# Weights in larger pieces and a re-planned start in a four-layer graph network kernel

## The chip, the cores and the metric

The kernel runs on one core of a Trainium2 chip. The metric is the device time of one execution in microseconds (us). The time before is the median of three runs; the profile is of one further execution. The engines are TensorE (PE; PEld is its loading of the stationary operand), VectorE (DVE), ScalarE (ACT), GpSimd (POOL) and SyncE (SP), which here only issues transfers (SPq).

## The reference

128 graphs of 128 nodes with 512 features pass four layers in float32. Each layer is `x = layernorm(x + f(x))`; the adjacency `adj` is the same in all four.

```python
# layer 0: Ah = adj + I, d = rowsum(Ah)**-0.5
f = relu((d * Ah * d) @ x @ W0 + b0)
# layer 1
q, k = split(x @ Wqk.T);  v = x @ Wv.T
w = softmax_over_nodes(sum((q @ k.T / 8) * adj, -1))
f = w * v
# layer 2
f = relu(concat([x, (adj @ x) / rowsum(adj)]) @ W2.T)
# layer 3: the d * Ah * d of layer 0
f = (d * Ah * d) @ (x @ W3 + b3)
```

## The kernel before

The graphs are worked on in 32 groups `t` of four. A group's x stays in one on-chip tile, `x_t`, through all four layers. Groups overlap: while group `t` is in layers 0 and 1, group `t - 1` is in layers 2 and 3.

Every product of 512 x 512 weights is done by `project` in a scheme with seven half-size products in place of eight (Strassen in Winograd's form). The weights' two row halves `h` and two column halves `j` give B11 (h=0, j=0), T1 (first loaded with the block h=0, j=1), B21 (h=1, j=0) and B22 (h=1, j=1); `weight_sums` makes T1, T2, T3 and T4 out of them in place, four subtractions for each weight, on VectorE for Wv and on GpSimd for the others. `left_sums` makes the matching sums of the left operand (`agg0s`, `xT1s`, `agg2s`, `xT2s`, `agg3s`). `project` emits the products in the order B11, B21, T1, T2, B22, T3 (layer 1 has B21 after T1), and T4 in a function `tail` that is kept in the list `tails` and runs within a later product. Three PSUM regions are used: B11 and B21 add up in the first, T1 and B22 in the second, T2, T3 and T4 in the third. ACT copies the first region (`s_o`, `s_v`) between B11 and B21, and VectorE reads the second and third (`u_o`, `u_v`) before the next product adds to them. `hooks` put other work behind a named product.

`w[:, k, c]` is the weight block of product `k` and row chunk `c`, 256 contiguous columns; each matrix is loaded in four blocks, for Wv and the x half of W2 (`turned`) each in four transfers of 32 partitions.

A matrix product needs its left operand transposed. `aggregate` gets that for free (x is the stationary operand, the transposed adjacency the moving one), and ACT copies the result from PSUM. Where x itself is wanted transposed, there are two ways: `turn_x` writes x to DRAM and reads it back in pieces (`xT1s`, `xT1y`), of which VectorE transposes blocks of 32 x 32; `turn_on_tensor` copies x on ACT, transposes it on TensorE by the identity, and ACT copies the result from PSUM. `begin` uses the second for group 0, `prep_transpose` for the adjacencies of groups 0 and 1; later adjacencies go through DRAM as well (`sa`, `ya`).

The order of work is set at build time. `Plan` records every operation; TensorE's order is that of the program text. `schedule` then lists the others one by one: for each engine, the ready operation with the earliest due time, by estimated durations. Its estimate for transfers is a latency LAND and one shared bus of BUS elements of 4 bytes per ns. At run time each engine takes its instructions strictly in the listed order and waits on semaphores. All transfers are issued on SyncE's one queue. All recorded operations carry line 266 in the profile.

Of the kernel before, what the change touches and what calls it, by code (L numbers as in the profile page):

```python
# [10 lines left out]
FP = mybir.dt.float32  # L11
AF = mybir.ActivationFunctionType
ALU = mybir.AluOpType
AX = mybir.AxisListType

P = 128
K = 32
Q = P // K
# [3 lines left out]
H = F // 2  # L22
# [103 lines left out]
class Plan:  # L126
# [4 lines left out]

    ENGINES = ("tensor", "vector", "scalar", "gpsimd", "sync")
    HOP = 200
    LAND, BUS = 1600, 95

    def __init__(self, nc, est):
        self.nc, self.est, self.ops, self.tags, self.group, self.dram = nc, est, [], {}, None, None
# [57 lines left out]
    def schedule(self):  # L195
        number = {op: i for i, op in enumerate(self.ops)}
        for (_, tag, bufs), tiles in self.tags.items():
            used = []
            for t in sorted((t for t in tiles if t.ops), key=lambda t: number[t.ops[0]]):
                if len(used) == bufs:  # L200
                    old = used.pop(min(range(bufs), key=lambda i: number[used[i].ops[-1]]))
                    assert number[old.ops[-1]] < number[t.ops[0]], (tag, bufs)
                    for op in t.ops:
                        if op.preds.isdisjoint(t.ops):
                            op.preds.update(old.ops)
                used.append(t)
        now = 0
        for op in self.ops:
            assert all(number[p] < number[op] for p in op.preds)
            for p in op.preds:  # L210
                p.succs.append(op)
            if op.engine == "tensor":
                op.last = now
                now += op.dur
        for op in reversed(self.ops):
            due = min([s.last - self.hop(op, s) for s in op.succs], default=now)
            op.last = min(op.last, due - op.dur)
        queue = {e: [] for e in self.ENGINES}
        waiting = {op: len(op.preds) for op in self.ops}
        free, bus, port = dict.fromkeys(self.ENGINES, 0), 0, 0  # L220
        pe = [op for op in self.ops if op.engine == "tensor"]
        for op in self.ops:
            if not op.preds:
                queue[op.engine].append((0, number[op], op))
        done = []
        while len(done) < len(self.ops):
            best = None
            for e in self.ENGINES:
                q = queue[e]
                if e == "tensor":  # L230
                    q = [c for c in q if c[2] is pe[0]]
                if not q:
                    continue
                q = [(max(c[0], port if c[2].port else 0),) + c[1:] for c in q]
                at = max(free[e], min(c[0] for c in q))
                pick = min((c for c in q if c[0] <= at), key=lambda c: (c[2].last, c[1]))
                for c in q:
                    if at < c[0] < at + pick[2].dur and c[2].last < at + pick[2].dur and c[2].last < pick[2].last:
                        pick, at = c, c[0]
                if best is None or at < best[0]:  # L240
                    best = at, e, pick[2]
            at, e, op = best
            queue[e] = [c for c in queue[e] if c[2] is not op]
            op.start, op.end = at, at + op.dur
            free[e] = op.end
            if op.port:
                port = op.end
            if e == "sync":
                bus = max(bus, op.end + self.LAND) + op.size / self.BUS
                op.lat = max(op.lat, bus - op.end)  # L250
            if e == "tensor":
                pe.pop(0)
            done.append(op)
            for s in op.succs:
                waiting[s] -= 1
                if not waiting[s]:
                    queue[s.engine].append((max(p.end + self.hop(p, s) for p in s.preds), number[s], s))
        return done
# [48 lines left out]
def kernel(  # L307
# [16 lines left out]
    last = NT - 1  # L324
# [31 lines left out]
    def weight(src, name, queue, turned=False):  # L356


        w = const.tile([P, 7, 2, H], FP, tag=name, name=name)
        for h in range(2):  # L360
            for j in range(2):
                s = src[:, j * H:(j + 1) * H]
                if turned:
                    s = s.rearrange("(b h c k) m -> h b k c m", b=Q, h=2, c=2)[h]
                    for b in range(Q):
                        queue.dma_start(w[b * K:(b + 1) * K, 2 * h + j], s[b])
                else:
                    queue.dma_start(w[:, 2 * h + j], s.rearrange("(h c p) m -> h p c m", h=2, c=2)[h])
        return w

    def weight_sums(w, eng):
        eng.tensor_tensor(w[:, T3], w[:, B22], w[:, T1], ALU.subtract)
        eng.tensor_tensor(w[:, T1], w[:, T1], w[:, B11], ALU.subtract)
        eng.tensor_tensor(w[:, T2], w[:, B22], w[:, T1], ALU.subtract)
        eng.tensor_tensor(w[:, T4], w[:, B21], w[:, T2], ALU.subtract)

    def broadcast_row(src, name, queue):
        r = const.tile([P, F], FP, tag=name, name=name)
# [136 lines left out]
    def project(name, t, parts, first, c11, fin, hooks=None, after=lambda: None, early=True,  # L515
                when=lambda f: f(), pairs=(0, 1)):

        hooks = hooks or {}  # L520
        qs = slice(pairs[0], pairs[-1] + 1)

        def region():
            return ps_b.tile([P, 2, H], FP, tag="pb", name=f"p_{name}_{t}")[:, qs]

        def operand(left_, k):
            s = st[left_, t]
            if isinstance(s, Ref):
                return s.rearrange("p (q r) (h c) n -> p q r h c n", r=2, h=2)[:, :, 0, (B11, B21).index(k)]
            return s[k]  # L530

        def product(p, k, fresh):
            with nc.unit():
                for q in pairs:
                    for i, (left_, w) in enumerate(parts):
                        for c in range(2):
                            nc.tensor.matmul(p[:, q - pairs[0], :], operand(left_, k)[:, q, c, :], w[:, k, c, :],
                                             start=(fresh and q == pairs[0] and i == 0 and c == 0),
                                             stop=(i == len(parts) - 1 and c == 1), skip_group_check=True)
            for f in hooks.get(k, ()):  # L540
                f()

        def block(tag):
            return tp.tile([P, 2, H], FP, tag=tag, name=f"{tag}_{name}_{t}", bufs=1 if tag in ("u5", "sb") else 2)[:, qs]

        g, q, v = region(), None, None
        product(g, B11, True)
        sa, sb = first(g, block)
        finish_tails()
        if early:  # L550
            product(g, B21, False)
            when(lambda: c11(g, block))
        q = region()
        product(q, T1, True)
        u5 = block("u5")
        nc.vector.tensor_tensor(u5, q, sb, ALU.add)
        if not early:
            product(g, B21, False)
            when(lambda: c11(g, block))
        v = region()  # L560
        product(v, T2, True)
        u2 = block("u2")
        nc.vector.tensor_tensor(u2, v, sb, ALU.add)
        product(q, B22, False)
        nc.vector.tensor_tensor(u2, q, u2, ALU.add)
        when(lambda: (fin(0, 1, u2), norm_stats(name, t, 0, pairs)))
        product(v, T3, False)
        nc.vector.tensor_tensor(u5, v, u5, ALU.add)
        fin(1, 1, u5)

        def tail():
            product(v, T4, False)
            nc.vector.tensor_tensor(sa, v, sa, ALU.add)
            fin(1, 0, sa)
            norm_stats(name, t, 1, pairs)
            after()

        tails.append(tail)
# [56 lines left out]
    def l0_agg(t, eng=nc.gpsimd, pairs=(slice(0, 2),)):  # L635
        left("agg0", t)
        for g in range(G):
            aggregate("agg0", t, g, st["anT", t])
        left_sums("agg0", t, eng, pairs)
# [189 lines left out]
    def begin():  # L829
# [3 lines left out]
        weight_sums(w0_sb, nc.gpsimd)  # L833
        l0_agg(0, nc.vector, ONE_BY_ONE)
        prep_rows(1)
        l0_out(0, {B11: [lambda: prep_transpose(1)], B22: [lambda: l0_agg(1)]})
        weight_sums(wv_sb, nc.vector)
        l0_out(1)
        l1_turn(0, turn_on_tensor, (0,))
# [3 lines left out]
        l1_qk(0, 1)  # L843
        for w in (w2x_sb, w2a_sb, w3_sb):
            weight_sums(w, nc.gpsimd)
        l1_turn(1)
        l1_out(0, {B11: [lambda: l1_scores(0)], B21: [lambda: l1_softmax(0)], T3: []})
        finish_tails()
        for r in range(2):
            l1_qk(1, r)  # L850
        l2_both(0, 0)

    def prep(t):
# [23 lines left out]
            l2_agg(t, 0)  # L877

    l2_both(last, 0)
    for q in range(2):  # L880
        l2_out(last, {B21: [lambda: l2_both(last, 1)]} if q == 0 else {}, (q,))
    for q in range(2):
        l3_agg_pair(last, q, nc.gpsimd)
        l3_bias(last, (2 * q, 2 * q + 1))
# [34 lines left out]
```

## Time and profile before

| | before |
|---|---|
| time, median of 3 runs | 2489.22 us (2488.04 to 2489.28) |
| span of the profiled execution | 2486.8 us |
| TensorE busy | 2457.3 us, 99% |
| VectorE, ScalarE, GpSimd busy | 73%, 39%, 54% |
| TensorE's share of the chain that ended last | 97% |
| moved by DMA | 243.34 MB, mean 98 GB/s |

In a row of a timeline the first number is the start in us from the start of the span, the second the length of the row (which may hold several instructions, xN); then the engine, the line, the operation, what it writes and reads, and, in brackets, the idle time of that engine before the row and what released it. A float32 matmul of the text counts as two in a row: the four of one product appear as x8.

The loads of the start stand in this order on the queue: adjacency 0, x of group 0, adjacency 1, W0, b0, x of group 1, Wqk, Wv, W2, then adjacency and x of group 2, W3, b3.

### The profile page before, as it was taken

What the parts mean: (1) busy time and instruction counts of PE and PEld (TensorE: products, weight loads), DVE (VectorE), ACT (ScalarE), POOL (GpSimd) and SP (SyncE); (2) the same over time, 40 slices, a digit from 0 to 9 for tenths busy, and PEclk for the clock granted to TensorE, in tenths of its full rate; (3) what the DMA queues carried; (4) which work ended last, traced back from release to release, by engine and by line L of the source; (5) the groups of instructions that cost most, each with busy time, mean ns of one, the idle gap of its engine ahead of it and who ended that gap; (6) DMA issues with size and microseconds to landing.
All of it is one profiled execution on the core that took longest, in us unless ns stands there. A gap on an engine that the chain in (4) does not pass through costs nothing.

```text
span 2486.8 us, 37083 instructions
## 1 busy us (share of the span) xinstructions
PE 2457.3 (99%) x13470; PEld 2206.9 (89%) x13470; DVE 1810.0 (73%) x3169; ACT 973.2 (39%) x1981; POOL 1334.0 (54%) x1522
## 2 busy tenths in 40 slices
PE   8899999999999999999999999999999999999998
PEld 7789988989999899899899998998898999989987
DVE  6677777777777777777777777777777777777665
ACT  2334434343344343343433443433434434443335
POOL 5446555555556464555555564645555555645443
PEclk9999999999999999999999999999999999999999
DMA  5333434333344324343243443343442434423220
GB/s 178 69 93 81 108 88 123 111 78 101 98 106 123 94 77 109 91 124 110 72 107 93 112 123 88 79 111 93 123 110 68 112 90 115 118 81 86 77 60 34
DMA packets 398805, 243.34 MB, mean 98 GB/s; under 512 B 140832, under 2 KB 365600, under 8 KB 398624
## 3 DMA queue, kind: packets, MB, share of 16 engines
q1 hardware_dynamic: 398624, 240.98, 36.2%
q8 instruction: 107, 1.75, 0.3%
q14 instruction: 74, 0.61, 0.1%
HBM read 127.66 MB, written 113.25 MB: 97 GB/s over the span
## 4 chain that ended last, share of the span: by engine, by line
PE 97%; SPq 1%; DVE 1%; DMA 1%; ACT 0%; issue 0%; POOL 0%; ACTq 0%; POOLq 0%; DVEq 0%
PE p_o L266 61%; PE p_v L266 16%; PE p_agg L266 14%; PE p_qk L266 5%; PE p_sc L266 1%; SPq L266 1%; DMA x<-in_x_dram 0%; DVE x L266 0%; PE p_ws L266 0%; ACT xT L266 0%; PE p_w L266 0%; DMA adj<-in_adj_dram 0%; PE p_xT L266 0%; ACT agg L266 0%; DVE wv_sb L266 0%
## 5 line engine op out<-in xcount | busy, mean ns | idle before, releaser
L266 ACT COPY agg<-p_agg 128x512 f32<-128x512 f32 x384 | 221.3, 584 | 573.1 <-PE p_agg L266 573.1
L266 PE MATMUL p_o<-w_sb,agg 128*128 128x256 f32 x1536 | 353.4, 379 | 0.5 <-DVE u_o L266 0.5
L266 PEld LDWEIGHTS p_o<-w_sb,agg 128*128 128x128 f32 x1536 | 286.7, 190 | 37.3 <-DVE u_o L266 0.9
L266 PE MATMUL p_o<-w2x_sb,xT2s 128*128 128x256 f32 x1024 | 263.0, 379 | 3.1 <-DVE xT2s L266 3.1
L266 PE MATMUL p_o<-w2a_sb,agg2s 128*128 128x256 f32 x1024 | 262.8, 379 | 0.0
L266 POOL TENSOR_TENSOR xT1s<-xT 128x512 f32<-128x512 f32 x64 | 94.1, 1471 | 290.2 <-DVE xT L266 220.1
L266 PE MATMUL p_agg<-anT,x 128*128 128x128 f32 x2048 | 243.9, 277 | 0.3 <-DVE anT L266 0.3
L266 PE MATMUL p_o<-w_sb,agg0s 128*128 128x256 f32 x1024 | 230.0, 383 | 7.0 <-DVE u_o L266 5.9
L266 PEld LDWEIGHTS p_agg<-anT,x 128*128 128x128 f32 x2048 | 235.4, 192 | 1.3 <-DVE anT L266 0.6
L266 PE MATMUL p_v<-wv_sb,xT1s 128*128 128x256 f32 x1024 | 233.3, 381 | 0.0
L266 POOL TENSOR_TENSOR agg3s<-agg 128x512 f32<-128x512 f32 x62 | 84.1, 1357 | 272.3 <-ACT agg L266 272.3
L266 PEld LDWEIGHTS p_o<-w_sb,agg0s 128*128 128x128 f32 x1024 | 193.5, 192 | 34.2 <-POOL mro L266 4.9
L266 PEld LDWEIGHTS p_o<-w2x_sb,xT2s 128*128 128x128 f32 x1024 | 194.4, 190 | 29.9 <-DVE xT2s L266 3.6
L266 PE MATMUL p_o<-w_sb,agg3s 128*128 128x256 f32 x992 | 219.2, 379 | 0.0
L266 PEld LDWEIGHTS p_o<-w2a_sb,agg2s 128*128 128x128 f32 x1024 | 194.6, 190 | 26.5
L266 PEld LDWEIGHTS p_v<-wv_sb,xT1s 128*128 128x128 f32 x1024 | 189.6, 190 | 27.3
L266 PEld LDWEIGHTS p_o<-w_sb,agg3s 128*128 128x128 f32 x992 | 188.5, 190 | 25.6
L266 ACT ACTIVATE x<-x,nmro,rstdo 128x512 f32<-128x512 f32 x257 | 198.7, 809 | 4.8 <-ACT nmro L266 0.3
L266 PE MATMUL p_o<-w2x_sb,xT 128*128 128x256 f32 x768 | 197.5, 380 | 1.2 <-ACT s_o L266 0.7
L266 PE MATMUL p_o<-w2a_sb,agg 128*128 128x256 f32 x768 | 197.1, 379 | 0.0
L266 DVE TENSOR_TENSOR u_o<-p_o,s_o 128x512 f32<-128x512 f32 (+1 forms) x132 | 89.2, 675 | 145.3 <-PE p_o L266 145.3
L266 PE MATMUL p_v<-wv_sb,xT 128*128 128x256 f32 x768 | 181.6, 379 | 0.9 <-DVE u_v L266 0.9
(141 smaller groups left out, 4662.1 us busy)
## 6 DMA issues: line engine op xcount, KB each, us to landing
x<-in_x_dram SPq DMA_DIRECT2D x31, 1024.0 KB, 5.1
xT1s<-x SPq DMA_DIRECT2D x124, 256.0 KB, 2.5
xT1y<-xT1s SPq DMA_DIRECT2D x248, 128.0 KB, 3.3
out_dram<-x SPq DMA_DIRECT2D x31, 1024.0 KB, 5.4
xT2s<-x SPq DMA_DIRECT2D x120, 256.0 KB, 2.6
xT2y<-xT2s SPq DMA_DIRECT2D x240, 128.0 KB, 2.8
sa<-ana SPq DMA_DIRECT2D x120, 128.0 KB, 3.3
ya<-sa SPq DMA_DIRECT2D x120, 128.0 KB, 3.2
```

What stands on the lines that cost most here:

```text
L266: getattr(getattr(self.nc, op.engine), method)(*[v.real() if isinstance(v, Ref) else v for v in args], **{k: v.real() if isinstance(v, Ref ...
```

## The change

The weights are laid by row chunk first (`w[:, c, k]`), so that the two column halves of a row lie side by side, and each transfer takes whole rows: half as many transfers, of twice the size, with runs of 2 KB in place of 1 KB. The planner's figures for transfers are changed (LAND 1800, BUS 62 elements or 248 bytes per ns, and at most FLIGHT 9 transfers in flight), which moves the order of operations on VectorE, ACT, GpSimd and SyncE. Group 1's x for layer 1 is transposed on TensorE, as group 0's is, and its place is behind T3 of layer 1 of group 0. The preparation of group 1's adjacency moves from behind B11 to behind B21. At the end, T4 of layer 3 of the last group but one is held back until the second half of the last group's layer 2 operands has been prepared.

```diff
-    LAND, BUS = 1600, 95
+    LAND, BUS, FLIGHT = 1800, 62, 9
...
+            if e == "sync" and len(landed) >= self.FLIGHT:
+                at = max(at, landed[-self.FLIGHT])
...
             if e == "sync":
                 bus = max(bus, op.end + self.LAND) + op.size / self.BUS
                 op.lat = max(op.lat, bus - op.end)
+                landed.append(op.end + op.lat)
...
-        w = const.tile([P, 7, 2, H], FP, tag=name, name=name)
+        w = const.tile([P, 2, 7, H], FP, tag=name, name=name)
         for h in range(2):
-            for j in range(2):
-                s = src[:, j * H:(j + 1) * H]
-                if turned:
-                    s = s.rearrange("(b h c k) m -> h b k c m", b=Q, h=2, c=2)[h]
-                    for b in range(Q):
-                        queue.dma_start(w[b * K:(b + 1) * K, 2 * h + j], s[b])
-                else:
-                    queue.dma_start(w[:, 2 * h + j], s.rearrange("(h c p) m -> h p c m", h=2, c=2)[h])
+            to = w[:, :, 2 * h:2 * h + 2].rearrange("p c j m -> p c (j m)")
+            if turned:
+                for b in range(Q):
+                    queue.dma_start(to[b * K:(b + 1) * K], src.rearrange("(b h c k) m -> h b k c m", b=Q, h=2, c=2)[h][b])
+            else:
+                queue.dma_start(to, src.rearrange("(h c p) m -> h p c m", h=2, c=2)[h])
...
-        l0_out(0, {B11: [lambda: prep_transpose(1)], B22: [lambda: l0_agg(1)]})
+        l0_out(0, {B21: [lambda: prep_transpose(1)], B22: [lambda: l0_agg(1)]})
...
-        l1_turn(1)
-        l1_out(0, {B11: [lambda: l1_scores(0)], B21: [lambda: l1_softmax(0)], T3: []})
+        l1_out(0, {B11: [lambda: l1_scores(0)], B21: [lambda: l1_softmax(0)],
+                   T3: [lambda: l1_turn(1, turn_on_tensor), lambda: l1_qk(1, 0)]})
         finish_tails()
-        for r in range(2):
-            l1_qk(1, r)
+        l1_qk(1, 1)
         l2_both(0, 0)
...
     l2_both(last, 0)
+    held = tails.pop()
     for q in range(2):
-        l2_out(last, {B21: [lambda: l2_both(last, 1)]} if q == 0 else {}, (q,))
+        l2_out(last, {B21: [lambda: l2_both(last, 1), held]} if q == 0 else {}, (q,))
```

The indices in `weight_sums` and in `project` follow the new layout.

## The prediction before the run

> **What bounds the kernel now.** I read the page first, then TensorE's own timeline, then all engines around its waits. The page gives the bound:
>
> ```profile
> PE 2457.3 (99%) x13470; PEld 2206.9 (89%) x13470; DVE 1810.0 (73%) x3169; ACT 973.2 (39%) x1981; POOL 1334.0 (54%) x1522
> ...
> PE 97%; SPq 1%; DVE 1%; DMA 1%; ACT 0%; issue 0%; POOL 0%; ACTq 0%; POOLq 0%; DVEq 0%
> ```
>
> TensorE is busy 2457.3 of 2486.8 us and is 97% of the chain that ended last. The order of its instructions is written out by hand, so the change can gain only where TensorE stands idle or runs slowly. Its timeline over the first 110 us has these waits (the bracket is the idle time before the row):
>
> ```profile
> 23.60 1.99 PE L266 MATMUL p_o<-w_sb,agg0s 128*128 128x256 f32 x8 [1.34 <-DVE u_o L266]
> ...
> 37.09 3.74 PE L266 MATMUL p_o<-w_sb,agg0s 128*128 128x256 f32 x16 [1.01 <-POOL agg0s L266]
> 45.37 6.32 PE L266 MATMUL p_o<-w_sb,agg0s 128*128 128x256 f32 x16 [4.53 <-DVE u_o L266]
> ...
> 77.66 5.44 PE L266 MATMUL p_qk<-wqk_sb,xT 128*128 128x128 f32 x32 [3.88 <-DVE xT L266]
> ...
> 90.44 1.13 PE L266 MATMUL p_o<-w2x_sb,xT 128*128 128x256 f32 x4 [0.68 <-ACT s_o L266]
> ...
> 98.33 1.13 PE L266 MATMUL p_o<-w2x_sb,xT2s 128*128 128x256 f32 x4 [1.51 <-DVE xT2s L266]
> ...
> 2439.57 1.13 PE L266 MATMUL p_o<-w2x_sb,xT2s 128*128 128x256 f32 x4 [1.58 <-DVE xT2s L266]
> ```
>
> With 1.56 at 15.59, 0.85 at 71.78 and smaller ones (0.35, 0.16, 0.24, 0.29) that is 16.4 us of idle TensorE between 1.34 and 98.33 us, then none until 2429. Two rows are also slow: 16 matmuls take 6.32 us at 45.37 where the same form takes 3.74 at 37.09, and 32 of 128 columns take 5.44 where 32 of p_agg take 3.73. The second half of each gap shows as a lower clock in the table of stretches: 0.83 for 40 to 60, against 1.00 in 20 to 40. Together 2.6 + 1.7 = 4.3 us. So some 21 us can be won at the start, and a few at the end; 2330 us between are matmuls without a gap.
>
> What makes the 4.53 us wait stands in the timeline of all engines:
>
> ```profile
> 30.93 0.69 DVE L266 TENSOR_TENSOR u_o<-p_o,u_o 128x512 f32<-128x512 f32 x1 [1.87 <-PE p_o L266]
> ...
> 35.92 0.69 DVE L266 TENSOR_REDUCE deg<-adj 128x4 f32<-128x512 f32 x1 [4.29 <-DMA adj<-in_adj_dram]
> ...
> 37.58 3.43 DVE L266 TENSOR_TENSOR wv_sb<-wv_sb 128x512 f32<-128x512 f32 x2
> ...
> 44.55 0.68 DVE L266 TENSOR_TENSOR u_o<-p_o,sb_o 128x512 f32<-128x512 f32 x1
> ```
>
> VectorE works in order. It stood 4.29 us at the row sums of group 2's adjacency, whose load sat behind 36 weight transfers on the one queue, and the read of p_o that frees TensorE came last. In the same way the 3.88 us wait ends with four VectorE block transposes of group 1's x, which come after the normalization of group 0.
>
> [...] its half-clock stretches last 6.83 and 3.41 us, and follow the gaps of 4.53 and 3.88, none of 1.6 or less. [...] wv_sb at 37.58 takes 1.7 us each beside GpSimd sums, x<-u_o 0.68 alone. [...] the first loads here land in the order of issue.
>
> **The change, part by part.** I compared the order of each engine's instructions before and after, and walked through the start with durations of the trace; times below are TensorE's, before and then after.
>
> *Weights in larger pieces.* The 36 wv and w2 transfers before adj become 18 with twice the bytes. Before, issues were 0.47 us apart (wv from 16.5 to 22.5). Eighteen take about 8.5 us from 16.5, so adj is issued near 25, not 33.0, and lands (2.9) near 28. TensorE's and GpSimd's operands are the same 256 contiguous columns. The first w0 half now goes ahead of group 1's adjacency: 0.26 MB lands per 0.7 us (9.8, 10.5 for the w0 pieces), so adj lands at 10.4, not 9.05. The prep of group 1 is therefore hooked after B21. No gain: B21 now waits for the copy of B11 (0.7), and the sums agg0s still finish at 21.1, because each VectorE sum alternates with a GpSimd weight sum (1.45 us a pair) until then.
>
> *First B22 product (23.60).* VectorE's order puts a pair of sums (0.75) and an addition to x (0.65) before the read that frees the region: 23.54 + 1.4 + 0.1, so 25.2. A loss of 1.6. T1 of group 1 follows after the same work (12.5 us, and no 1.01 wait as only one weight sum stands before agg0s): 37.09 to 37.7.
>
> *Second B22 (45.37).* adj no longer blocks and one wv sum instead of two stands in the way. VectorE: T3 read from 32.5; x 34.9; wv 36.3; deg 37.0; s_o 37.7; small ones 38.2; x beside GpSimd 39.9; statistics 40.6; read 41.2. TensorE arrives at 37.7 + 3.45 = 41.2. The 4.53 wait and its slow clock go: 51.52 becomes 44.65 and, the same work following, p_ws (70.71) becomes 63.85.
>
> *Group 1's x on TensorE.* Adds 16 transposes: 8 take 1.04 us alone, 0.95 in a row, so 1.9 us. It takes away four block transposes (2.49) and twelve transfers. But T4 of layer 1 needs VectorE's last read of v, which now stands after group 0's additions and statistics: ws 64.3, two from p_v 65.4, two from u_v beside GpSimd 68.4 (2.96 before), statistics 69.9, read 70.6. TensorE would be there at 68.0. So T4 70.6 against 71.78, and layer 2's first aggregation 74.1 against 82.94. After that three waits grow, since their causes moved less than TensorE: ACT's copies of xT (0.29 to about 0.9; 86.05 to 77.8), s_o, now queued behind a normalization and two copies (0.68 to 1.2; 90.44 to 82.7), and xT2s. For the last, VectorE now has group 2's block transposes of ya ahead of agg2s. In before, ana was done at 87.6 and ya issued until 93.8, landing 3.2 later: 9.4 us. Ana is done at 78.6 now, ya lands near 88.0, and six instructions of 0.7 follow: 92.2 for 98.33, with a gap of 3.1 where 1.51 was. **Gain at the start 6.1 us.**
>
> *New figures for the planner.* They change the order on VectorE, GpSimd, ACT and the queue in every one of the some 29 steady periods of 76.1 us. I set the new places against what TensorE waits for at 1200 to 1276: the second half of xT for layer 1 is transposed at about 1254 instead of 1250.1, used at 1259.4; its sum s1 is ready at 1256.4, used at 1263.7; xT2s s1 moves from 1228.2 to 1228.6, used at 1236.7; a store of 1 MB (5.4) now goes ahead of xT1y, still in time. The least slack is some 2.5 us. Nothing.
>
> *The held tail.* T4 of group 30's layer 3 (1.73 us) moves into the 1.58 us gap before 2439.57. But it had hidden ACT's copy s_o, which B21 now waits for (0.6 to 0.7, like 90.44). Net **0.9 us**.
>
> Sum 7.0 us: 2489.2 - 7.0 = **2482.2**.
>
> **The rivals.** *Within 0.2%:* the new waits (3.1 before B22, 2.6 at T4, 3.1 at xT2s) [...] one of them a little longer costs its excess and about 2 us at half clock. Or ya lands 2 us later. Gain 2 to 5: about 2485.5. For it: two of three such gaps did this before. [...] 25%. *More:* ya lands early enough that xT2s waits 1.5 as before (1.6 more), the additions in front of T4 run without GpSimd (1.5), s_o fits at the end (0.6): 2478.5. For it: VectorE's order beside GpSimd decides. Against: all three at once. 7%. *Slower:* one new wait in each steady period, such as xT1y behind the store. At 0.5 us more than its slack in 29 periods it is 14.5 - 7.0: 2497. For it, the one queue is shared and VectorE blocks in order; against, slack of 2.5 us or more at each use. 6%.
>
> **How the numbers follow.** Forecast 62%, within 25%, more 7%, slower 6%. "Faster by over 0.2%" is below 2484.2: 62 + 7, 69%. The range takes in the forecast with the bounds of its unknowns: below, the case of more, 2478.5; above, a clock loss of 2 and ya 3 us late, 2487.5.
>
> **What would show it.** Right: in the trace of after no wait over 1 us between 26 and 60, clock 1.00 there; a wait near 3 at the first B22; one near 2.6 at T4 of layer 1 released by u_v; one near 3 at xT2s, at about 92; then none until 2420; the sums of wv shorter. Wrong: VectorE waiting for adj or ya over 2 us before agg2s, a half clock in the first 100 us, or any TensorE wait that recurs every 76 us.

## The result and the profile after

The change made the kernel slower: 2507.73 us (median of six runs, 2506.91 to 2511.80) against 2488.66 us for the kernel before on the same chip (six runs). The ratio is 1.0079, with a 95% interval of 1.0066 to 1.0092. The forecast was 2482.2 us.

From the page of the kernel after (where the recorded operations carry line 269), the busy time of the engines, the chain of work that ended last by engine, and the same chain by line:

```profile
PE 2461.5 (98%) x13486; PEld 2203.1 (88%) x13486; DVE 1849.0 (74%) x3165; ACT 967.9 (39%) x1989; POOL 1320.1 (53%) x1522
...
PE 90%; DVE 7%; ACT 1%; DMA 1%; issue 1%; SPq 0%; POOL 0%; ACTq 0%; DVEq 0%; POOLq 0%
PE p_o L269 61%; PE p_agg L269 14%; PE p_v L269 10%; PE p_qk L269 4%; DVE u_v L269 1%; DVE dh L269 1%; PE p_sc L269 1%; DVE w L269 1%; DVE rs L269 1%; DVE deg L269 1%; ACT e L269 0%; DMA x<-in_x_dram 0%; DVE x L269 0%; DVE scr L269 0%; SPq L269 0%
```

TensorE's busy time grew by only 4.2 us, but its share of the chain fell from 97% to 90%, and VectorE came in with 7%. The lines name the place: `w`, `rs`, `deg`, `dh`, `u_v` are VectorE's work around the scores and the softmax of layer 1, and VectorE's 7% of the span, some 175 us, is more than a start of 100 us can hold. Something recurs. TensorE's timeline shows it (start, length, and in brackets the idle time before the row):

```profile
25.02 1.99 PE L269 MATMUL p_o<-w_sb,agg0s 128*128 128x256 f32 x8 [2.74 <-DVE u_o L269]
...
69.37 1.99 PE L269 MATMUL p_v<-wv_sb,xT 128*128 128x256 f32 x8 [1.92 <-DVE u_v L269]
...
89.96 1.13 PE L269 MATMUL p_o<-w2x_sb,xT2s 128*128 128x256 f32 x4 [2.78 <-DVE xT2s L269]
...
197.62 1.97 PE L269 MATMUL p_v<-wv_sb,xT1s 128*128 128x256 f32 x8 [0.79 <-DVE u_v L269]
...
274.79 1.96 PE L269 MATMUL p_v<-wv_sb,xT1s 128*128 128x256 f32 x8 [0.81 <-DVE u_v L269]
```

Up to 90 us all goes well. The waits of 4.53 and 3.88 us are gone, the clock is 1.00 in each stretch of 20 us, and the product with xT2s starts at 89.96 where it started at 98.33: 8.4 us gained. Then a wait of 0.8 us that the kernel before did not have comes back every 77.17 us, 27 times, the last at 2204.11.

The balance can be drawn from the rows of `p_w`, the transpose in layer 1's softmax, which each period has once. Averaged over 23 periods, two of them stand 76.13 us apart before and 77.17 after. Of the 15 groups of matmuls in a period 14 take the same time within 0.005 us; one, p_v with xT1s, goes from 7.06 to 8.11. So 27 x 1.045 = 28.2 us are lost and 8.4 won at the start; from the last row of `p_w` to the end of the span it is 81.2 us before and 80.1 after, so 1.2 is won at the end. That leaves 18.6, the difference of the two spans (2505.4 and 2486.8).

What makes the wait stands in the timeline of all engines of the kernel after, around one of them (some rows of ScalarE, and those of the weight loads, are left out):

```profile
1193.84 1.27 POOL L269 TENSOR_TENSOR agg0s<-agg 128x512 f32<-128x512 f32 x1
1194.05 1.07 DVE L269 TENSOR_TENSOR w<-w,dm 128x4 f32<-128x4 f32 x1
...
1195.18 1.27 POOL L269 TENSOR_TENSOR agg0s<-agg0s,agg 128x512 f32<-128x512 f32 x1
1195.23 1.44 DVE L269 TENSOR_TENSOR rs<-rs,d 128x4 f32<-128x4 f32 x2
1196.38 0.27 PE L269 MATMUL p_w<-ident,w 128*4 128x128 f32 x1
1196.48 3.62 PE L269 MATMUL p_v<-wv_sb,xT1s 128*128 128x256 f32 x16
1196.53 1.27 POOL L269 TENSOR_TENSOR agg0s<-agg,agg0s 128x512 f32<-128x512 f32 x1
1196.58 0.69 DVE L269 TENSOR_TENSOR u_v<-p_v,s_v 128x512 f32<-128x512 f32 x1
1197.19 0.67 DVE L269 TENSOR_REDUCE deg<-adj 128x4 f32<-128x512 f32 x1
1197.76 1.26 POOL L269 TENSOR_TENSOR agg0s<-agg 128x512 f32<-128x512 f32 x1
1197.90 1.16 DVE L269 TENSOR_SCALAR dh<-deg 128x4 f32<-128x4 f32 x1
...
1200.01 0.15 DVE L269 RECIPROCAL rsum<-ssum 4x1 f32<-4x1 f32 x1 [0.43 <-ACT e L269]
1200.09 0.66 DVE L269 TENSOR_TENSOR u_v<-p_v,s_v 128x512 f32<-128x512 f32 x1
...
1200.89 1.97 PE L269 MATMUL p_v<-wv_sb,xT1s 128*128 128x256 f32 x8 [0.79 <-DVE u_v L269]
```

The product at 1200.89 is T3. It adds to the region that T2 filled (the first half of the x16 row), so it waits for VectorE to read T2, the u_v at 1200.09. T2 was done over a microsecond before, but in VectorE's fixed order that read stands behind the whole softmax. And on the way there, operations on 128x4 elements take over a microsecond (`w`, the two `rs` together, `dh`), and each gets done about when one of GpSimd's sums agg0s ends: `w` at 1195.12 and the sum at 1195.11, `dh` at 1199.06 and the sum at 1199.02. Here is the same stretch in the timeline of the kernel before:

```profile
1262.48 1.27 POOL L266 TENSOR_TENSOR agg0s<-agg,agg0s 128x512 f32<-128x512 f32 x1
...
1264.93 0.16 DVE L266 TENSOR_TENSOR w<-w,dm 128x4 f32<-128x4 f32 x1
1264.96 1.28 POOL L266 TENSOR_TENSOR agg0s<-agg 128x512 f32<-128x512 f32 x1
...
1265.20 1.25 DVE L266 TENSOR_TENSOR rs<-rs,d 128x4 f32<-128x4 f32 x2
...
1267.25 0.27 PE L266 MATMUL p_w<-ident,w 128*4 128x128 f32 x1
...
1267.69 0.17 DVE L266 TENSOR_SCALAR dh<-deg 128x4 f32<-128x4 f32 x1
...
1269.29 0.69 DVE L266 TENSOR_TENSOR u_v<-p_v,s_v 128x512 f32<-128x512 f32 x1 [0.34 <-PE p_v L266]
```

Before, GpSimd has done three of the four sums when the scores arrive and does only one beside them. After, all four lie there. Counted from `p_w`, the read of T2 comes at 2.04 us before (and waits 0.34 for TensorE) and at 3.71 after. The extra length in these two periods is 0.91 for `w`, 0.19 for `rs` and 0.99 for `dh`, together 2.09, of which `rsum` shows 2.08. The read of T2 had 0.4 us of that in hand and T3 another 0.7, so T3 starts 1.0 us later, of which 0.8 stands as a wait in its row.

The period of before that is shown is the rarer kind. In 23 of its 32 groups the single sum meets `w` (0.92 to 1.28 us), in four an `rs`, as here:

```profile
L266 DVE TENSOR_TENSOR w<-w,dm 128x4 f32<-128x4 f32 x32 | 25.3, 790 | 1.1
```

(busy time, mean ns of one, idle before). So in most groups one of these operations is long before, and three are after.

The theory to be tested (A): the new figures moved GpSimd's sums over VectorE's small operations, and these collide. The rivals: another part of the change, such as the weights' layout, stretches the period (B); VectorE is late because `deg` waits for adj or the second half of xT is transposed later, and the sums have nothing to do with it (C).

### The profile page after: what moved, and what is told of

It reads as the page before. It is cut to its first block, busy times and chain, and to the rows that moved or that the text cites. A ratio compares the mean times of both kernels' runs of the same rounds, so it can differ in the third digit from the quotient of the medians.

```text
span 2505.4 us, 37051 instructions
## 1 busy us (share of the span) xinstructions
PE 2461.5 (98%) x13486; PEld 2203.1 (88%) x13486; DVE 1849.0 (74%) x3165; ACT 967.9 (39%) x1989; POOL 1320.1 (53%) x1522
## 4 chain that ended last, share of the span: by engine, by line
PE 90%; DVE 7%; ACT 1%; DMA 1%; issue 1%; SPq 0%; POOL 0%; ACTq 0%; DVEq 0%; POOLq 0%
PE p_o L269 61%; PE p_agg L269 14%; PE p_v L269 10%; PE p_qk L269 4%; DVE u_v L269 1%; DVE dh L269 1%; PE p_sc L269 1%; DVE w L269 1%; DVE rs L269 1%; DVE deg L269 1%; ACT e L269 0%; DMA x<-in_x_dram 0%; DVE x L269 0%; DVE scr L269 0%; SPq L269 0%
## 5 line engine op out<-in xcount | busy, mean ns | idle before, releaser
L269 POOL TENSOR_SCALAR rstdo<-mvo 128x2 f32<-128x2 f32 (+1 forms) x131 | 29.8, 228 | 536.0 <-DVE mvo L269 533.3
L269 PE MATMUL p_v<-wv_sb,xT1s 128*128 128x256 f32 x1024 | 239.7, 383 | 21.8 <-DVE u_v L269 21.8
L269 DVE TENSOR_TENSOR u_o<-p_o,u_o 128x512 f32<-128x512 f32 (+1 forms) x196 | 131.8, 673 | 121.0 <-PE p_o L269 120.8
```

The source lines that it names most:

```text
L269: getattr(getattr(self.nc, op.engine), method)(*[v.real() if isinstance(v, Ref) else v for v in args], **{k: v.real() if isinstance(v, Ref ...
```

## The experiments

Every number below is a median in us with the ratio to the kernel before on the same chip and its 95% interval. "p_w to p_ws" is the distance of these two rows on TensorE in a steady period: it is 5.39 when T3 does not wait, and 6.41 to 6.45 after.

### The figures alone, and all but the figures

First the change with the planner's figures of before:

```diff
-    LAND, BUS, FLIGHT = 1800, 62, 9
+    LAND, BUS, FLIGHT = 1600, 95, 10 ** 9
```

> The kernel after with the planner's figures of before (LAND 1600, BUS 95, no FLIGHT); weights' layout, group 1 on TensorE and the held tail stay. Theory A (GpSimd's four agg0s sums, placed by the new figures over VectorE's small operations of layer 1, make the recurring wait p_v <- u_v of 0.80 us): the sums go back to three before and one after the scores, no wait recurs in the steady periods, the period is 76.1 us again, and the start keeps some 6 to 8 us of gain: 2479 to 2484 us. Rival B (another part of the change, such as the weights' row chunks read by TensorE or the additional transposes, stretches each period): the wait stays and the time is 2505 or more.

Measured: 2491.26, 1.0012 (1.0006 to 1.0019). p_w to p_ws is 5.38 or 5.39 in every period; nothing recurs. So B falls: the other parts of the change make no recurring wait. (Two single waits of p_w for `rs`, 0.82 and 1.71 us, stand in this profile; their cause is open.) But the time is 7 us above what was expected: the start's gain is gone as well, which no theory had said. The product with xT2s starts at 97.61. From the timeline of all engines of e1:

```profile
26.28 0.38 SPq L269 DMA_DIRECT2D adj<-in_adj_dram  x1
...
32.03 0.69 DVE L269 TENSOR_REDUCE deg<-adj 128x4 f32<-128x512 f32 x1 [6.47 <-DMA adj<-in_adj_dram]
...
38.85 6.17 PE L269 MATMUL p_o<-w_sb,agg 128*128 128x256 f32 x16 [6.99 <-DVE u_o L269]
```

The larger pieces do bring adj forward (issued at 26.28 instead of 33.02, landed at 32.01 instead of 35.90), but in the order made with the old figures `deg` stands earlier on VectorE too, presumably since the planner believes in a still earlier landing; VectorE blocks for 6.47 us instead of 4.29, and TensorE waits 6.99.

Then the opposite, the kernel before with the new figures and nothing else:

```diff
-    LAND, BUS = 1600, 95
+    LAND, BUS, FLIGHT = 1800, 62, 9
```

> The kernel before with the new figures and nothing else of the change. Theory A: the wait of 0.8 us before a product of layer 1 recurs some 27 times and the period is 77.2 us: 27 x 1.05 = 28 us more than before, give or take 4 for the reordered start, so 2513 to 2521 us. Rival B: no recurring wait, 2484 to 2492.

Measured: 2509.30, 1.0085 (1.0070 to 1.0100). The wait of 0.8 recurs 27 times and the period is 77.17. The time lies below the expected range, which had allowed the start 4 us: it gains 6.6 (xT2s at 91.70). From the timeline of all engines of e2:

```profile
33.80 0.38 SPq L269 DMA_DIRECT2D adj<-in_adj_dram  x1
...
43.04 0.69 DVE L269 TENSOR_TENSOR u_o<-p_o,sb_o 128x512 f32<-128x512 f32 x1 [0.24 <-PE p_o L269]
43.64 0.68 DVE L269 TENSOR_REDUCE deg<-adj 128x4 f32<-128x512 f32 x1
```

adj is issued as late as before, but `deg` now stands behind the reads that TensorE needs, and the long wait is gone. 2488.55 - 6.6 + 27 x 1.045 = 2510. The new figures alone explain both the gain at the start and the loss later.

### Only GpSimd's order

The third and fourth sum are moved behind the operation that makes `d`, in the finished list. No other engine's order changes, and no figure.

```diff
-        for op in self.schedule():
+        for op in later(self.schedule()):
...
+def later(ops):
+    rows = {f"agg0s{i}_{t}": f"d_{t + 2}" for t in range(3, 30) for i in (3, 4)}
+    held = {}
+    for op in ops:
+        if op.engine == "gpsimd" and name_of(op) in rows:
+            held.setdefault(rows[name_of(op)], []).append(op)
+            continue
+        yield op
+        if op.engine == "gpsimd" and name_of(op) in held:
+            yield from held.pop(name_of(op))
```

> The kernel after with one thing changed: on GpSimd the third and fourth agg0s sum of groups 3 to 29 go behind the power that makes d two groups later, that is behind the softmax of layer 1. Every other engine keeps its order. Theory A: dh takes 0.17 us in place of 1.16, u_v comes about 1 us earlier, the recurring wait is 0 to 0.1 us, the period 76.1: 2478 to 2483 us. w and one rs stay long (1.07 and about 1.3), which the slack takes up. Rival C (VectorE's order is late because deg stands in it and waits for adj, or since the second half of xT is transposed later): the wait of 0.8 stays, 2504 to 2510.

Measured: 2482.18, 0.9977 (0.9968 to 0.9987), some 25 us less than the kernel after. VectorE's order is that of after, with `deg` and xT where they were, so C falls. Three groups of VectorE's table (busy time, mean ns of one, idle before) tell which collision counted. The kernel after:

```profile
L269 DVE TENSOR_TENSOR rs<-rs,d 128x4 f32<-128x4 f32 x64 | 41.6, 650 | 2.2
L269 DVE TENSOR_SCALAR dh<-deg 128x4 f32<-128x4 f32 x32 | 32.5, 1016 | 1.1
L269 DVE TENSOR_TENSOR w<-w,dm 128x4 f32<-128x4 f32 x32 | 31.9, 997 | 1.1
```

and e3:

```profile
L269 DVE TENSOR_SCALAR dh<-deg 128x4 f32<-128x4 f32 x32 | 6.4, 199 | 1.1
L269 DVE TENSOR_TENSOR w<-w,dm 128x4 f32<-128x4 f32 x32 | 31.9, 997 | 1.1
L269 DVE TENSOR_TENSOR rs<-rs,d 128x4 f32<-128x4 f32 x64 | 41.6, 650 | 2.2
```

`w` and `rs` are as long as after; of the operations ahead of the read of T2, `dh` alone changed, from 1016 to 199 ns. (`e` behind it meets a moved sum and grows from 268 to 722, which T3 does not wait for.) In the kernel before, the means are 790 (`w`), 221 (`rs`) and 199 (`dh`). Here two collisions nearly fit into the slack; the third is the one that TensorE feels. p_w to p_ws is 5.44, so 0.05 us is still felt.

With the second sum moved too:

> The kernel with two sums later (e3), and the second agg0s sum later too, so that one sum is left over the scores. rs takes 0.15 us each, u_v comes 1.3 us earlier. e3 still loses 0.05 us a period between p_w and p_ws (5.44 against 5.39): 27 x 0.05 to 0.07 = 1.5 to 1.9 us less, 2480.5, if the later sums collide with nothing; 2482 to 2484 if they collide with VectorE's additions to x and that is felt.

Measured: 2480.41, 0.9971 (0.9961 to 0.9981); p_w to p_ws is 5.39 and the period 76.13, as before the change. The sums collide with nothing that is felt in their later place.

### Which figure

```diff
-    LAND, BUS, FLIGHT = 1800, 62, 9
+    LAND, BUS, FLIGHT = 1800, 95, 9
```

> The kernel after with BUS back at 95 alone (LAND 1800 and FLIGHT 9 stay). The planner then puts one sum ahead of the normalization and three over the scores. Theory A, by its own arithmetic: three sums hit w and rs (1.1 us together) and end before dh, u_v is 0.6 us late against a slack of 0.9: no recurring wait, or at most 0.2 us; 2479 to 2486 us. If any sum over the scores were enough, or if LAND were the cause, the wait would be near 0.8 again: 2503 to 2510.

Measured: 2494.70, 1.0028 (1.0017 to 1.0039). `dh` is short (173 ns) as expected, but each of the two `rs` now meets a sum of its own (1101 ns each, `w` 308), and p_w to p_ws is 5.62: 27 x 0.235 = 6.3 us, and 1.05 more in one group, so the time is 9 us above what was expected. Most of the rest is the start, where a wait of 6.6 us for u_o at 38 is back (xT2s at 95.76). So with LAND 1800 and FLIGHT 9 kept it is BUS, the low rate of the transfers, that mends the start, and BUS also that puts the fourth sum beside `dh`. Whether BUS at 62 does it without the other two was not run.

### What it is in dh that waits

`dh` is `deg + 1`, with a single operand in on-chip memory, and the collisions that the prediction counted are of operations with two (`wv_sb`, 1.7 us each beside GpSimd's sums). So `dh` was computed on GpSimd, and `dm`, of the same kind, follows `deg`:

```diff
-        nc.vector.tensor_scalar(dh, deg, 1.0, None, ALU.add)
+        nc.gpsimd.tensor_scalar(dh, deg, 1.0, None, ALU.add)
```

> The kernel after (all four sums over the scores) with dh computed on GpSimd, so that dm follows deg on VectorE. If a VectorE tensor_scalar with one input waits for the running GpSimd sum, the delay moves to dm (1.1 us in place of 0.15) and the recurring wait stays at 0.7 to 0.8: 2505 to 2510 us. If the 1 us belonged to dh alone (its handing over to GpSimd), dm takes 0.15 and the wait is gone: 2480 to 2484.

Measured: 2512.75, 1.0095 (1.0078 to 1.0112), with 6.56 from p_w to p_ws; it is above the expected range, but the wait stayed. From the timeline of all engines of e9:

```profile
1125.61 1.27 POOL L269 TENSOR_TENSOR agg0s<-agg 128x512 f32<-128x512 f32 x1
1125.74 1.16 DVE L269 TENSOR_SCALAR dm<-deg 128x4 f32<-128x4 f32 x1
```

The delay has moved to `dm` (0.16 in the kernel after). It belongs to the kind of operation and the place, not to `dh`. Then both on GpSimd:

```diff
-        nc.vector.tensor_scalar(dm, deg, DEG_EPS, None, ALU.max)
+        nc.gpsimd.tensor_scalar(dm, deg, DEG_EPS, None, ALU.max)
```

> The kernel after with dh and dm both on GpSimd, behind the sums; VectorE goes from deg to mx and nmx, a tensor_scalar of 4x1. If only the count of elements or the copying forms on 128 lanes collide, nmx takes 0.14, u_v comes 1 us earlier and the wait is gone: 2480 to 2484. If any tensor_scalar that reads SBUF waits for the running sum, nmx takes up to 1 us until the fourth sum ends (about 0.8 us after nmx could start), u_v gains only 0.2 to 0.3, and a wait near 0.5 stays: 2495 to 2503.

Measured: 2484.10, 0.9986 (0.9979 to 0.9993), p_w to p_ws 5.39 (5.54 once). From the timeline of all engines of e10:

```profile
1112.33 1.27 POOL L269 TENSOR_TENSOR agg0s<-agg 128x512 f32<-128x512 f32 x1
...
1112.66 0.14 DVE L269 TENSOR_SCALAR nmx<-mx 4x1 f32<-4x1 f32 x1
```

All four sums still lie over the scores here, and the wait is gone. (The start has two new waits for `ana`, 3.73 and 1.85 us, since `dm` comes late there.) The tensor_scalar of 4x1 that follows runs beside the fourth sum without delay.

### The parts of the start and the end

Each of these takes one part out of e3 (2482.18 and 0.9977; e3 ran on another chip than these three, so ratios are compared).

The held tail left out:

```diff
-    held = tails.pop()
...
-        l2_out(last, {B21: [lambda: l2_both(last, 1), held]} if q == 0 else {}, (q,))
+        l2_out(last, {B21: [lambda: l2_both(last, 1)]} if q == 0 else {}, (q,))
```

> The kernel with two sums later (e3), and without the held tail. By the prediction's step the tail was worth 0.9 us: 2483.1 us. By the waits of the kernel after (the new s_o wait is 0.46, the removed one before T1 of the last group 1.58) it is 1.1: 2483.3. If the tail moved work without gain, 2482.2 as before it.

Measured: 2483.59, 0.9984 (0.9978 to 0.9991). The intervals of the ratios overlap. In the profiles, the stretch from the last group's first product of layer 2 with xT to the end of the span is 56.7 us long without and 55.7 with the held tail: 1.0 us. The wait of 1.57 comes back, the one of 0.46 for s_o goes.

Group 1's x through memory, as before:

```diff
+        l1_turn(1)
-        l1_out(0, {B11: [lambda: l1_scores(0)], B21: [lambda: l1_softmax(0)],
-                   T3: [lambda: l1_turn(1, turn_on_tensor), lambda: l1_qk(1, 0)]})
+        l1_out(0, {B11: [lambda: l1_scores(0)], B21: [lambda: l1_softmax(0)], T3: []})
...
-        l1_qk(1, 1)
+        for r in range(2):
+            l1_qk(1, r)
```

> The kernel with two sums later (e3), and group 1's x for layer 1 through device memory as before. By the prediction the transposes on TensorE cost 1.9 us of work and a wait of 2.6, and save a wait of 3.88 and 1.7 of slow clock and bring the rest forward: without them the wait before p_qk comes back at 2.4 to 3.9 us with half clock behind it, 2483 to 2485. The kernel with the new figures alone reached the xT2s product of layer 2 at 91.70, though, against 92.46 in e3: if group 1 on TensorE is worth nothing, 2481 to 2482.5.

Measured: 2483.21, 0.9981 (0.9974 to 0.9988). The median lies in the range that was expected if the transposes matter, but the interval takes in e3's ratio. In the profiles the product with xT2s starts at 90.81, earlier than e3's 92.46. A wait of 2.50 us before p_qk returns without a half clock, and the 16 transposes and the larger wait for u_v go: no gain from the transposes shows, and one of about 1 us is not excluded.

The weights in the pieces of before (`w[:, k, c]`, four blocks for each matrix, in e3):

> The kernel with two sums later (e3), and the weights in the pieces of before (seven blocks ahead of the row chunk, twice as many transfers of half the size). The prediction gave the smaller number of transfers the whole 4.53 us wait and its slow clock, as adj then lands near 28: without it 2487 to 2489. Rival: the new figures alone place adj's sum later on VectorE, and the wait is gone without the layout, as in the kernel with new figures alone: 2481 to 2484.

Measured: 2481.83, 0.9979 (0.9971 to 0.9986). Not told apart from e3 either; xT2s starts at 88.94. The layout and the larger pieces bring nothing that shows.

### Two ways to keep the gain without the loss

The new figures only for transfers that are planned within the first 100 us:

```diff
-    LAND, BUS, FLIGHT = 1800, 62, 9
+    LAND, BUS, FLIGHT = 1600, 95, 9
...
-                bus = max(bus, op.end + self.LAND) + op.size / self.BUS
+                land, rate = (1800, 62) if at < 100_000 else (self.LAND, self.BUS)
+                bus = max(bus, op.end + land) + op.size / rate
```

> The kernel after with the new figures for transfers planned in the first 100 us alone, and 1600 and 95 later and in the due times: the start's order is that of after, the steady order that of before. No recurring wait, period 76.13, the start's gain of 6 to 8 us and the held tail: 2480 to 2482 us, as good as e8. If the start's gain hung on the steady order or the due times, 2484 or more.

Measured: 2480.88, 0.9973 (0.9962 to 0.9984), period 76.13. This and e8 beat both kernels by some 7 and 27 us.

And the new figures throughout, with a planner that counts these collisions:

```diff
-    return 160 + (1.12 if len(both) > 1 else 1.04) * n, 0, 0, len(both) > 1 and n > 32
+    return 160 + (1.12 if len(both) > 1 else 1.04) * n, 0, 0, len(both) > 1 or (method == "tensor_scalar" and len(both) == 1)
```

> The kernel after with its new figures, and one line of the planner's estimate changed: it counts VectorE's small operations with two inputs and its tensor_scalar from on-chip memory as users of what GpSimd's sums use, so it plans them as waiting. The four sums stay over the scores; VectorE's order becomes deg, mx, nmx, dh, dm, rdeg, u_v, so dh's wait (to the end of the fourth sum, some 0.6 us now) runs beside ACT's exponential. By the trace of after, u_v comes 0.6 to 0.7 us earlier: the recurring wait falls from 0.8 to 0.1 or 0.2 us and the time to 2482 to 2487 us. If the order on VectorE were not what counts, 2505 or more.

Measured: 2487.03, 0.9996 (0.9987 to 1.0004), at the far end of what was expected. The planner now puts `mx` and `nmx` ahead of `dh`, as foreseen, and p_w to p_ws falls to 5.59; the remaining 0.2 us, 27 times, are 5.6 us. Most of the loss is avoided, though the sums stay where they are.

## Why the prediction was wrong

The step that failed is "New figures for the planner": "The least slack is some 2.5 us. Nothing." It cost 27 x 1.045 = 28.2 us. The working there took moved operations and asked whether their own results still came in time. agg0s, which is not among them, does: its last sum ends at 1199.03 and is first used at 1227.45. What the working did not ask is whom a moved operation delays where it now stands. The slack that counted, 0.7 us between the read of T2 and T3, is not in its list either. The prediction had the collision in hand, since it read it off wv_sb (1.7 us each beside GpSimd's sums), and it listed "any TensorE wait that recurs every 76 us" as the sign of failure; it did not apply the one to the other in the steady period. Its rival "slower" had the right form, a small new wait in each period, but the wrong cause (xT1y behind the store), a size of 0.5 instead of 1.05, and 6%.

There was a second gap under it. The collisions that the prediction counted are of operations with two inputs in on-chip memory. `dh` has one, and it took 1.16 us beside a sum, 0.17 alone; it was this one-input operation that took the last of the slack. The stretch of the kernel before around the 4.53 us wait already held a case: `dm` there takes 0.62 us and ends at 42.15, when a GpSimd sum has ended at 42.13. And the prediction's x<-u_o, "0.68 alone", was not alone: it starts at 36.98, and a sum that starts at 37.12 takes 1.67 where others take 1.27, which fits GpSimd being the one held up there.

The rest, by its steps:

| | before | predicted | after |
|---|---|---|---|
| first B22, wait | 23.60, 1.34 | 25.2, about 3 | 25.02, 2.74 |
| T4 of layer 1, wait | 71.78, 0.85 | 70.6, 2.6 | 69.37, 1.92 |
| B21 of layer 2, wait | 90.44, 0.68 | 82.7, 1.2 | 80.80, 0.75 |
| product with xT2s, wait | 98.33, 1.51 | 92.2, 3.1 | 89.96, 2.78 |
| held tail | | gains 0.9 | gains 1.0 (e5 against e3) |

*The start's gain* was right in size: 6.1 predicted, 8.4 in the profile of after, 5.9 in that of e3, which has a stretch at half clock. The waits came out somewhat shorter than worked out. For the first B22 the prediction's own terms, 23.54 + 1.4 + 0.1, give 25.0 and not 25.2; 25.02 was measured. The sum of everything but the failed step, 2482.2, is what e3 measured (2482.18); the agreement to a tenth is luck, as the next point shows.

*Its cause* was wrong. The prediction gave the long wait's end to the smaller number of transfers: "Eighteen take about 8.5 us from 16.5, so adj is issued near 25". It is issued at 24.66, but it lands at 31.07, 6.4 us later and not 2.9; and that is not why VectorE stopped blocking. e7 has the old transfers (adj lands at 36.08) and the gain; e1 has the new ones and a longer block than before. What goes with the gain is the place of `deg` in VectorE's order, which the figures set: in e7 it starts at 40.56, behind reads of p_o, while in the kernel before, in e1 and in e4 VectorE blocks at it for 4.29 to 7.03 us. No run moved `deg` alone. So the one part that was called "Nothing" made both the gain and the loss, and the part that was given the gain made neither.

*Group 1 on TensorE* was counted as part of the gain; e6 shows none beyond the noise.

*The clock:* no half clock in the first 100 us of after, as predicted. The rival "within 0.2%" feared that waits of 2.6 to 3.1 us would bring it. In some executions they do: the eight matmuls after the wait before the first B22 take 1.99 us in after and 3.58 in e8. Both waits were 2.74 us, so the length of a wait alone does not decide; the last section has more cases.

Open: why GpSimd's sums lie later was read from the orders alone. With the low rate the planner puts the transposes of the second half of xT behind VectorE's statistics of the group in layer 2, so xT1s and then agg0s start later. No run tried that link by itself.

## What to carry to other kernels

When a scheduler's figures change, check each moved operation twice: whether it is still in time, and what stands beside it now on an engine whose operations a trace shows to be longer beside it (here `dh`, 1.16 us against 0.17). Follow the delay through the in-order queue to the next read that frees TensorE; a microsecond there, 27 times, outweighs everything won once at the start. And test the parts one by one even when the sum comes out right, since a figure and a layout that were made for the same wait need not both be at work.

## What was not expected of the hardware

- A VectorE tensor_scalar with one input on 128x4 took 1.16 us beside a GpSimd sum and 0.17 alone (`dh`): it ended at 1199.06, the sum at 1199.02. `dm` in e9 took 1.16 as well, against 0.16 in after. On 4x128 (`e`) one took 0.80 beside a sum in e3 and 0.27 alone. On 4x1 (`nmx`) it took 0.14 beside a sum in e10. Why that one was not longer was not shown; it is one shape.
- A tensor_reduce was not delayed: `deg` took 0.67 with sums running through it (1197.19 in after), 0.68 with none (1266.98 in the kernel before). Nor was u_v, which reads one operand from PSUM: 0.69 with a sum at 1196.53, 0.69 at 1269.29 without.
- The same wait of 2.6 to 2.8 us before the first B22 was followed by a slow clock in some executions and not in others: the mean from 20 to 40 us was 1.00 in after and e11, 0.91 in e3 and e8, 0.83 in e2. Worked out from these means, the stretches at half clock are about 3.6 us long in e3 and 6.8 in e2; half of that, about 1.8 or 3.4 us, is lost by this estimate.
- Other waits show no order by length either. After one of 1.99 us in e10 the eight matmuls at 73.20 took 2.86 us; after one of 1.92 us in after the same eight, at 69.37, took 1.99. After the longer waits before the product with xT2s, 2.78 us in after and 3.21 in e6, its four matmuls took 1.13, as after 0.40 us at 76.33 in after. What else goes with the slow clock was not shown.
- adj needed 2.9 us from issue to VectorE in the kernel before (33.02 to 35.92) and 5.8 in e1 (26.28 to 32.03), where it was issued 7 us earlier, with more of the weights' bytes still under way: at its issue seven weight transfers of 128 KB or more had not landed, against five of 64 KB in the kernel before.
